# A Macaron layer on one core: the front of the second router pass starts during the first attention, and two groups of instructions are pinned in the order

## The chip, the cores and the metric

The kernel runs on one core of one Trainium2 chip. A core has a matrix engine (TensorE, PE in the profile, with its weight loads listed as PEld), a vector engine (VectorE, DVE), a scalar engine (ScalarE, ACT), a general engine (GpSimd, POOL), and a sync engine (SyncE, SP) that issues DMAs. The metric is the time of one execution on the device in microseconds (us); lower is better. All data are float32.

## The reference

The input x is 2 sequences of 2048 tokens with 256 channels. The layer is a half-weighted feed-forward part, a causal attention, and the same feed-forward part again with the same weights:

```python
x = x + 0.5 * ffn(layernorm(x))
x = x + attn(layernorm(x), Wq, Wk, Wv, Wo)      # causal, d_k = 128
x = x + 0.5 * ffn(layernorm(x))

def ffn(x):
    xln = ln(x, ln1_w, ln1_b)
    state = xln @ Ws
    x = x + sigmoid(xln @ Wr) * (xln @ Wv) @ Wo
    h = ln(x, ln2_w, ln2_b)
    conf = concat(sigmoid(h @ conf_rwkv.T), sigmoid(h @ conf_trans))   # three experts
    bids = conf * capital_shares * sigmoid(h @ w_diff) + h @ W_aff
    winners = argmax(bids)
    scale = conf[winner] / (conf[winner] + 1e-6)
    out_rw[e] = square(relu(h @ K[e])) @ V[e]          # e = 0, 1; hidden size 1024
    out_gt = (h @ W1 * sigmoid(state @ W2)) @ W3       # the third expert
    return x + select(winners, out_rw[0], out_rw[1], out_gt) * scale
```

The reference computes all experts for all tokens and selects. The kernel sends each token to its winner alone.

## The kernel before, in words

**Tiling.** A tile is 128 tokens on the partitions. A group is 512 tokens (4 tiles, `TB`), a sequence is 4 groups (`GB`). The kernel works on *segments*, one for each sequence and feed-forward part: s0 and s1 in the first part, t0 and t1 in the second. An expert block is 256 tokens (`BLK`).

**The front** (`front`, L747, with `Group`, from L374) does everything of a feed-forward part that comes ahead of the experts. For each group: `start` takes the mean and variance of x with bn_stats and bn_aggr on DVE and has POOL raise them to the power -0.5 (L291), a first guess that two DVE steps refine; `norm1` normalizes and copies x into the token's row (a DMA on SP, L404); `columns` transposes on PE (`ps_t`); `r` and `v` multiply by w_r and w_v (L362, result `ps_p`), take the sigmoid on ACT and form `gate_t` on DVE (L432); `mix` multiplies by w_o (L442, result `acc`); `route` forms the router's sums in two parts (`ps_rc`, copied to `by_col` by ACT); `deviation` and `norm2` are the second norm; `logits` and `choose` find the winner (`wins` on DVE, L525); `rank` counts on PE the tokens ahead (`ps_rank`, L536); `slot` makes each token's place; `move` scatters the group's rows to `by_slot` in device memory with four indirect DMAs from POOL (L567). The generator interleaves these steps over neighbouring groups: group n's choice stands beside group n+1's projections and the start of group n+2. After a segment's last group `finish` makes a steering table (`ps_n`, `steer`) that tells the experts where their blocks begin.

A `Group` has two flags. With `by_exp` the sigmoid of the gate is taken as a tanh on ACT with an extra scale and shift on DVE; with `conf_by_exp` the sigmoid of the confidences is an exp on ACT with an add and a reciprocal on DVE. Both let groups that run beside the softmax use the same activation table as its exp. The `by_exp` argument of `front` says up to which group this holds.

**The experts** (`experts`, L829) run over a list of `Block`s: gt blocks (the third expert), rw blocks (the first two) and half blocks. SP reads a block's place out of the steering table and loads its rows (`rows_in`, `load_rows`) and, for rw, its weights (`w_k`, `w_e`). `ready` scales a row on DVE (L975) and normalizes it on ACT; `columns` transposes on PE (`ps_bt`, L846); `first` multiplies by the expert's first matrix (L862) and forms `hid` or `gated` (L994) on DVE; `second` multiplies back (`acc`, L877), and the result rows `res` (L902) are scattered from POOL (L910). The rows of block n+1 are made ready within block n.

**Attention** (`attention`, L1067) takes one sequence. `qkv` transposes and projects; `scores` multiplies queries by keys (`ps_s`, L1125), finds the row maximum on DVE (L1134) and the exp on ACT (`prob`, L1141); `values` transposes the probabilities (`ps_pt`, L1165), copies them to SBUF alternately on ACT (L1170) and DVE (L1172) as `p_tr`, and multiplies by v (`ps_o`, L1178); `sums` copies `ps_o` to `o_t` (L1194), multiplies by Wo (`ps_out`, L1200) and adds into x. Group n of a sequence is final once its `sums` are done; the scores of group n+1 are interleaved with the values of group n.

**What sets the order.** The parts are Python generators. Their interleaving gives the order in which instructions are traced; a scheduler then orders each engine's instructions by priority and readiness as it estimates them, so an instruction can move ahead of others traced before it. Two calls hold one back: `tc.keep_in_program_order(ins)` keeps it behind everything traced before it on its engine, and `tc.issue_after(ins)` keeps it behind a given instruction. Only the first feed-forward part's first front is laid out by hand (`tc.manual_schedule`) on PE, DVE and ACT.

The whole program runs: the front of s0; the front of s1 interleaved with the experts of the first part; x read back from device memory (`x_mid`) with its statistics (`normed`, L1286, through `normalize` and `moments`); a conditional block (L1056) that is normally skipped; the first attention on t0; the second attention on t1 with the front of t0 between its steps; the experts of the second part, with the front of t1 between them. `advance(steps, n)` takes n steps of a generator, `run` takes all, `interleave(main, side, steps, every)` takes `steps` steps of the side for each `every` of the main.

In the kernel before, the lines that place the second front are these (8 front steps for each 9 steps of the second attention, then the rest until t0 is placed, then 10 steps more):

```python
        run(attention(work, t0["x"], [r[:, :, YN : YN + C] for r in t0["rows"]]))
        following = front(front_pool, [t0, t1], by_exp=GB)
        interleave(attention(work, t1["x"]), until_placed(following, t0), 9, 8)
        advance(following, AHEAD)
```

Of the kernel before, what the change touches and what calls it, by code (L numbers as in the profile page):

```python
# [17 lines left out]
C = 256  # L18
# [37 lines left out]
def run(steps):  # L56
    for _ in steps:
        pass
# [20 lines left out]
def kernel(ctx: ExitStack, tc: tile.TileContext, a: dict, out: bass.AP):  # L79
    nc = tc.nc  # L80
    x_in = a["x"].flatten_outer_dims()
    out = out.flatten_outer_dims()
    B, T, _ = a["x"].shape
# [192 lines left out]
    def moments(src, landing=False):  # L276

        stats = small.tile([P, TB, 6], F32, name="stats")
        mv = small.tile([P, TB, 2], F32, name="mv")
        for t in range(TB):  # L280
            ins = nc.vector.bn_stats(stats[:, t, :], src[:, t, :])
            if landing and t == 0:
                tc.keep_in_program_order(ins)
        for t in range(TB):
            nc.vector.bn_aggr(mv[:, t, :], stats[:, t, :])
        return mv
# [81 lines left out]
    groups = []  # L368

# [3 lines left out]
    class Group:  # L373
# [136 lines left out]
        def choose(self):  # L510
# [14 lines left out]
            nc.vector.scalar_tensor_tensor(  # L525
                wins[:, 1, :], wins[:, 0, :], 1.0, wins[:, 2, :], ALU.is_lt, ALU.subtract
            )
# [52 lines left out]
    def segment(b, bufs, prior=None, waited=False):  # L580
# [5 lines left out]
        if prior is None:  # L586
# [4 lines left out]
            "moves": groups[-1], "prior": prior, "waited": waited,  # L591
# [155 lines left out]
    def front(work, segs, by_exp=-1, on_move=lambda: None, fill=()):  # L747
# [3 lines left out]
            Group(work, seg, n, (b * GB + n <= by_exp, b * GB + n < by_exp)) for b, seg in enumerate(segs) for n in range(GB)  # L751
        ]

# [6 lines left out]

        todo[0].start()
        run(todo[0].norm1(TB // 2))
        yield
        todo[1].start()
# [8 lines left out]
        for i, this in enumerate(todo):  # L773
# [19 lines left out]
            if further:  # L793
                further.start()
                yield
# [33 lines left out]
    def experts(work, segs, dest, redo=None):  # L829
# [118 lines left out]
        class Block:  # L948
# [36 lines left out]
            def first(self, following=None):  # L985

                if self.kind == "gt":
# [3 lines left out]
                    if following:  # L991
                        following.ready()
# [22 lines left out]
        def pipelined(todo):  # L1015
# [8 lines left out]
            todo[0].ready()  # L1024
            todo[0].columns()
            yield
            for i, block in enumerate(todo):
# [4 lines left out]
                yield from block.first(todo[i + 1] if i + 1 < len(todo) else None)  # L1032
# [34 lines left out]
    def attention(work, x, normed=()):  # L1067

        stat = work

# [120 lines left out]
        def sums(n, ps_o, probs):  # L1191
# [4 lines left out]
            for t0 in range(0, TB, 2):  # L1196
# [6 lines left out]
                for i in range(2):  # L1203
                    t = t0 + i
                    nc.vector.scalar_tensor_tensor(
                        x[n][:, t, :], ps[:, i, :], probs[t][1], x[n][:, t, :], ALU.mult, ALU.add
                    )
            yield
# [106 lines left out]
    with pool("attention", "right") as work:  # L1315
# [4 lines left out]
        run(attention(work, t0["x"], [r[:, :, YN : YN + C] for r in t0["rows"]]))  # L1320
        following = front(front_pool, [t0, t1], by_exp=GB)
        interleave(attention(work, t1["x"]), until_placed(following, t0), 9, 8)
# [50 lines left out]
```

## Time and profile before

| what | value |
|---|---|
| time, median of 3 runs | 898.68 us (897.06 to 899.32) |
| profiled execution | 900.5 us, of which span 898.5 us |
| mean granted PE clock over the span | 0.988 |
| DVE, ACT, POOL busy | 467.4, 320.1, 184.8 us |
| q1 (hardware DMA queue) / q0 (software queue) | 29.0% / 9.5% of 16 engines |
| HBM read and written | 82.47 and 38.68 MB |

The span is the time from the first to the last instruction that the profiler records; the time of an execution is some 2 us more. Busy time is summed over an engine's instructions; matmuls are pipelined, so their printed durations overlap and the distance between starts tells what one costs. In the listings, L12 is line 12 of the kernel, `out<-in` names the tiles, x4 the number of instructions. In a table of stretches each row is one stretch: its bounds and length, then for PE, PEld, DVE, ACT and POOL the busy us and (in brackets) the instructions, then the granted clock of PE, the DMA share and the mean GB/s. In a list of waits, each line gives the waiting instruction, the instruction that released it, and total us, number and mean of the waits.

By the trace, the first feed-forward part's last expert block ends at 338.7 us, the first attention runs from 342.3 to 466.5 us (its first `ps_out` at 395.9), the second with the front of t0 from 466.5 to 637.6 us, and the first rw block of the second part starts at 702.2 us.

### The profile page before, as it was taken

How to read it: one execution, taken by the hardware profiler on the slowest of the kernel's cores; microseconds unless marked ns; L12 is line 12 of the kernel's file. 1: busy time of each engine (PE TensorE's matmuls, PEld its weight loads, DVE VectorE, ACT ScalarE, POOL GpSimd, SP SyncE). 2: the span in 40 equal slices, each digit the busy share in tenths (PEclk: the TensorE clock that was granted, in tenths of full speed). 3: DMA queues.
4: the chain of work that ended last, by engine and by line, in shares of the span. 5: the costliest groups of instructions: out<-in, count | busy, mean ns of one | idle time of the engine just before them, and what ended most of it. 6: DMA issues, size and time to landing. Idle time of an engine off the chain costs nothing. (4 is left out here: it accounts for less than half of the span.)

```text
span 898.5 us, 12471 instructions
## 1 busy us (share of the span) xinstructions
PE 846.5 (94%) x4136; PEld 616.5 (69%) x4136; DVE 467.4 (52%) x1857; ACT 320.1 (36%) x694; POOL 184.8 (21%) x232
## 2 busy tenths in 40 slices
PE   6999899999999998899899999999899899999996
PEld 4556467788878895545456556556566688888885
DVE  3688757333345445478532687675776532333322
ACT  3332541324344332344533344442352223243221
POOL 3145245111032211000000102022323410122101
PEclk9999999999999999999999999999999999999998
DMA  9425637647188543000000001021375654539642
GB/s 308 150 102 194 224 142 264 216 136 264 49 293 296 171 142 100 0 1 1 0 1 1 1 0 71 24 95 42 127 279 182 242 191 161 177 95 333 199 164 70
DMA packets 66370, 123.71 MB, mean 138 GB/s; under 512 B 4718, under 2 KB 44526, under 8 KB 66288
## 3 DMA queue, kind: packets, MB, share of 16 engines
q1 hardware_dynamic: 55856, 87.46, 29.0%
q0 software_dynamic: 8384, 33.70, 9.5%
q10 hardware_dynamic: 2048, 1.58, 0.6%
q8 instruction: 37, 0.61, 0.3%
q14 instruction: 45, 0.37, 0.1%
HBM read 82.47 MB, written 38.68 MB: 135 GB/s over the span
## 5 line engine op out<-in xcount | busy, mean ns | idle before, releaser
L877 PE MATMUL acc<-w_e,hid 128*128 128x256 f32 x704 | 158.2, 382 | 0.0
L862 PE MATMUL ps_b<-cols,w_k 128*128 128x256 f32 (+1 forms) x768 | 157.3, 363 | 0.0
L862 PEld LDWEIGHTS ps_b<-cols,w_k 128*128 128x128 f32 x768 | 137.4, 191 | 17.1
L877 PEld LDWEIGHTS acc<-w_e,hid 128*128 128x128 f32 x704 | 132.7, 192 | 17.9 <-DVE hid L1004 0.6
L291 POOL TENSOR_TENSOR r<-ve,mhalf 128x4 f32<-128x4 f32 (+1 forms) x40 | 50.9, 1272 | 383.0 <-DVE ve L332 264.4
L1003 ACT ACTIVATE relu<-ps_b 128x512 f32<-128x512 f32 x88 | 52.0, 591 | 179.5 <-PE ps_b L862 155.9
L1004 DVE TENSOR_TENSOR hid<-ps_b,relu 128x512 f32<-128x512 f32 x88 | 60.8, 691 | 84.8 <-ACT relu L1003 79.3
L902 DVE SCALAR_TENSOR_TENSOR res<-acc,rows_in 128x256 f32<-128x256 f32 x68 | 30.0, 478 | 123.9 <-PE acc L877 123.9
L1178 PE MATMUL ps_o<-p_tr,v 128*128 128x512 f32 (+3 forms) x160 | 75.2, 554 | 4.7 <-DVE p_tr L1172 1.9
L567 POOL DMA_INDIRECT by_slot<-rows,slots x64 | 62.5, 977 | 32.0 <-issue 27.0
L1141 ACT ACTIVATE prob<-ps_s,shift 128x512 f32<-128x512 f32 (+2 forms) x80 | 49.0, 621 | 53.8 <-DVE shift L1138 44.5
L1125 PE MATMUL ps_s<-k_t,q_t 128*128 128x512 f32 (+3 forms) x160 | 64.8, 533 | 0.9 <-ACT prob L1141 0.9
L910 POOL DMA_INDIRECT out_dram<-res,where x34 | 33.6, 987 | 155.4 <-DVE res L902 142.3
L362 PE MATMUL ps_p<-y_t,w_r 128*128 128x512 f32 x128 | 63.5, 615 | 0.8 <-ACT y_t L416 0.7
L362 PE MATMUL ps_p<-y_t,w_v 128*128 128x512 f32 x128 | 62.2, 605 | 0.0
L910 POOL DMA_INDIRECT x_mid<-res,where x34 | 33.7, 992 | 133.2 <-DVE res L902 128.0
L442 PE MATMUL acc<-w_o,gate_t 128*128 128x256 f32 x256 | 60.1, 385 | 0.6 <-DVE gate_t L432 0.6
L1165 PEld LDWEIGHTS ps_pt<-ident,prob 128*128 128x128 f32 x272 | 34.1, 143 | 36.9 <-issue 18.8
L1134 DVE TENSOR_REDUCE top<-ps_s 128x1 f32<-128x512 f32 (+2 forms) x80 | 48.4, 607 | 17.2 <-PE ps_s L1125 15.8
L442 PEld LDWEIGHTS acc<-w_o,gate_t 128*128 128x128 f32 x256 | 47.1, 190 | 8.6 <-DVE gate_t L432 1.4
L1125 PEld LDWEIGHTS ps_s<-k_t,q_t 128*128 128x128 f32 x160 | 29.9, 193 | 32.8 <-issue 24.7
L354 ACT ACTIVATE cols<-ps_bt,lnp 128x256 f32<-128x256 f32 (+1 forms) x96 | 47.2, 554 | 13.2 <-PE ps_bt L846 12.9
(219 smaller groups left out, 1128.1 us busy)
## 6 DMA issues: line engine op xcount, KB each, us to landing
w_k<-in_K_rwkv_dram SPq DMA_DIRECT2D x24, 1024.0 KB, 5.3
w_e<-in_V_rwkv_dram SPq DMA_DIRECT2D x24, 1024.0 KB, 5.8
rows_in<-by_slot SPq DMA_DIRECT2D x20, 516.0 KB, 6.6
rows_in<-by_slot SPq DMA_DIRECT2D x12, 772.0 KB, 6.6
rows<-in_x_dram SPq DMA_DIRECT2D x8, 512.0 KB, 5.9
by_slot<-rows_in SPq DMA_DIRECT2D x3, 772.0 KB, 10.5
x_mid<-rows_in SPq DMA_DIRECT2D x1, 2048.0 KB, 15.8
rows<-x_mid SPq DMA_DIRECT2D x4, 512.0 KB, 5.1
```

Of the source, the lines that this page charges most:

```text
L291: guess = nc.gpsimd.tensor_tensor(r0[:, 0:n, :], ve[:, 0:n, :], mhalf[:, 0:n, :], ALU.pow)
L362: nc.tensor.matmul(ps, lhsT=w[:, k, m * P : (m + 1) * P], rhs=src_t[:, k, :], start=k == 0, stop=k == KC - 1)
L442: nc.tensor.matmul(acc[:, i, :], lhsT=self.gate_t[:, k, t * P : (t + 1) * P], rhs=w_o[:, k, :], start=k == 0, stop=k == KC - 1,)
L567: nc.gpsimd.indirect_dma_start(out=by_slot, out_offset=bass.IndirectOffsetOnAxis(ap=self.slots[:, t : t + 1], axis=0), in_=self.rows[:, t, :],
L862: nc.tensor.matmul(ps[:, j, :], lhsT=w[:, k, (m0 + j) * P : (m0 + j + 1) * P], rhs=cols[:, k, :], start=k == 0, stop=k == KC - 1,)
L877: nc.tensor.matmul(acc[:, i, :], lhsT=src[:, j, i * P : (i + 1) * P], rhs=w[:, j, :], start=j == 0, stop=j == n - 1,)
L910: ins = nc.gpsimd.indirect_dma_start(out=dest, out_offset=bass.IndirectOffsetOnAxis(ap=where[:, i : i + 1], axis=0), in_=res[:, i, :], in_ ...
L1003: nc.scalar.activation(relu, ps, AF.Relu)
L1004: self.made = nc.vector.tensor_mul(self.mid[:, j : j + step, :], ps, relu).ins
L1125: nc.tensor.matmul(ps[:, :w], lhsT=seq["q_t"][:, qi * P : (qi + 1) * P], rhs=seq["k_t"][:, c * TG : c * TG + w], start=True, stop=True,)
L1141: nc.scalar.activation(prob[:, c * TG : c * TG + w], ps[:, :w], AF.Exp, bias=shift, scale=ATTN_SCALE, accum_out=sums[:, c : c + 1],)
L1178: nc.tensor.matmul(ps_o[:, i0 * P :], lhsT=seq["v"][:, j, :], rhs=p_tr[:, i0 * P :], start=j == 0, stop=j == blocks - 1,)
```

## The change

In words:

1. In `moments`, all four bn_stats of statistics taken with `landing=True` (those of the x that is read back from `x_mid`) are kept in program order, not the first alone.
2. The front keeps in `lately["chosen"]` the last instruction of the latest `choose`. The first block of the experts, and the block that is made ready within the first block, are made ready behind that instruction on DVE.
3. Each segment has a counter `attended`. It is 4 (all groups) by default; for t0 and t1 it starts at 0 and attention raises it after each group's `sums`. The front starts a group only when the counter is past it, and otherwise yields a step.
4. The front of t0 and t1 is created ahead of the first attention. It advances on every second step of the first attention and on every step of the second, then runs until t0 is placed, and then 10 steps more as before.
5. The groups that use tanh for the gate are now all of t0 and the first three of t1 (before: t0 and the first of t1); those that use exp for the confidences are t0 and the first of t1 (before: t0). The front of the first part uses neither, as before.

```diff
@@ -279,7 +279,7 @@
         mv = small.tile([P, TB, 2], F32, name="mv")
         for t in range(TB):
             ins = nc.vector.bn_stats(stats[:, t, :], src[:, t, :])
-            if landing and t == 0:
+            if landing:
                 tc.keep_in_program_order(ins)
         for t in range(TB):
             nc.vector.bn_aggr(mv[:, t, :], stats[:, t, :])
@@ -366,6 +366,7 @@
 
 
     groups = []
+    lately = {}
 
 
     RW_AT, GT_AT, HALF_AT, MORE_AT, STEER = accumulate(POS, POS, POS, SQ, 1)
@@ -522,9 +523,9 @@
             wins = self.wins = sort_pool.tile([P, E, TB], F32, name="wins")
             nc.vector.tensor_tensor(wins[:, 0, :], bids[:, 0, :], most[:, 1, :], ALU.is_ge)
             nc.vector.tensor_tensor(wins[:, 2, :], bids[:, 2, :], most[:, 0, :], ALU.is_gt)
-            nc.vector.scalar_tensor_tensor(
+            lately["chosen"] = nc.vector.scalar_tensor_tensor(
                 wins[:, 1, :], wins[:, 0, :], 1.0, wins[:, 2, :], ALU.is_lt, ALU.subtract
-            )
+            ).ins
             for t in range(TB):
                 at = self.n * TB + t
                 nc.vector.tensor_add(upto[:, :, at + 1], upto[:, :, at], wins[:, :, t])
@@ -588,7 +589,7 @@
         groups.append(f"moves{b}_{len(groups)}")
         return {
             "b": b, "ids": ids[:, b, :], "bufs": bufs, "rows": [], "in_rows": [], "x": [], "upto": upto, "moved": [],
-            "moves": groups[-1], "prior": prior, "waited": waited,
+            "moves": groups[-1], "prior": prior, "waited": waited, "attended": GB,
         }
 
     def finish(seg):
@@ -744,12 +745,17 @@
         nc.vector.reduce_max(at[:, 5:6], flags, axis=AX.X)
         nc.vector.tensor_copy(steer[:, MORE_AT : MORE_AT + 1], at[:, 5:6])
 
-    def front(work, segs, by_exp=-1, on_move=lambda: None, fill=()):
+    def front(work, segs, by_exp=-2, on_move=lambda: None, fill=()):
+
 
 
         todo = [
-            Group(work, seg, n, (b * GB + n <= by_exp, b * GB + n < by_exp)) for b, seg in enumerate(segs) for n in range(GB)
+            Group(work, seg, n, (b * GB + n < by_exp + 2, b * GB + n < by_exp)) for b, seg in enumerate(segs) for n in range(GB)
         ]
+
+        def attended(group):
+            while group.seg["attended"] <= group.n:
+                yield
 
         def at(i):
             return todo[i] if 0 <= i < len(todo) else None
@@ -758,9 +764,11 @@
             group.move()
             on_move()
 
+        yield from attended(todo[0])
         todo[0].start()
         run(todo[0].norm1(TB // 2))
         yield
+        yield from attended(todo[1])
         todo[1].start()
         todo[0].columns()
         yield
@@ -791,6 +799,7 @@
                 yield
 
             if further:
+                yield from attended(further)
                 further.start()
                 yield
             if late:
@@ -982,14 +991,14 @@
                     self.cols_y = columns(self.rows, YN, 0)
                 self.cols = columns(self.rows, X1, 1)
 
-            def first(self, following=None):
+            def first(self, following=None, early=False):
 
                 if self.kind == "gt":
                     sig = work.tile([P, 2, BLK], F32, name="gt_sig", bufs=1)
                     nc.scalar.activation(sig, several(w_s2, 0, self.cols_y), AF.Sigmoid)
                     yield
                     if following:
-                        following.ready()
+                        following.ready(lately["chosen"] if early else None)
                     self.mid = work.tile([P, KC, BLK], F32, name="gated", bufs=2)
                     self.made = nc.vector.tensor_mul(self.mid, several(later["w_1"], 0, self.cols), sig).ins
                     yield
@@ -1021,7 +1030,8 @@
 
             yield
             yield
-            todo[0].ready()
+
+            todo[0].ready(lately["chosen"])
             todo[0].columns()
             yield
             for i, block in enumerate(todo):
@@ -1029,7 +1039,7 @@
                     todo[i + 1].load_weights()
                 if i + 2 < len(todo):
                     todo[i + 2].load_rows()
-                yield from block.first(todo[i + 1] if i + 1 < len(todo) else None)
+                yield from block.first(todo[i + 1] if i + 1 < len(todo) else None, i == 0)
                 if i + 1 < len(todo):
                     todo[i + 1].columns()
                     yield
@@ -1064,9 +1074,10 @@
                 run(redo())
 
 
-    def attention(work, x, normed=()):
+    def attention(work, seg, normed=()):
 
         stat = work
+        x = seg["x"]
 
         def qkv(made):
             q_t = work.tile([P, T], F32, name="q_t")
@@ -1205,6 +1216,7 @@
                     nc.vector.scalar_tensor_tensor(
                         x[n][:, t, :], ps[:, i, :], probs[t][1], x[n][:, t, :], ALU.mult, ALU.add
                     )
+            seg["attended"] += 1
             yield
 
         seq, probs, left = {}, [], []
@@ -1317,9 +1329,13 @@
             x = front_pool.tile([P, TB, C], F32, name=f"x{n}")
             wait_for(nc.sync.dma_start(x, token_tiles(x_mid, GB + n)).ins, s0["results"] + s1["results"])
             t1["x"].append(x)
-        run(attention(work, t0["x"], [r[:, :, YN : YN + C] for r in t0["rows"]]))
-        following = front(front_pool, [t0, t1], by_exp=GB)
-        interleave(attention(work, t1["x"]), until_placed(following, t0), 9, 8)
+        t0["attended"] = t1["attended"] = 0
+        following = front(front_pool, [t0, t1], by_exp=GB + 1)
+        for n, _ in enumerate(attention(work, t0, [r[:, :, YN : YN + C] for r in t0["rows"]])):
+            advance(following, n % 2)
+        for _ in attention(work, t1):
+            advance(following, 1)
+        run(until_placed(following, t0))
         advance(following, AHEAD)
     expert_pool = ctx.enter_context(pool("experts1", "right"))
     main = experts(expert_pool, [t0, t1], out)
```

## Prediction

> **What bounds the kernel now.** I read the page's first part and its chain first, then a table of stretches around the two attentions, then PE's waits in each stretch, and last how the change reorders each engine's instructions.
>
> ```profile
> PE 846.5 (94%) x4136; PEld 616.5 (69%) x4136; DVE 467.4 (52%) x1857; ACT 320.1 (36%) x694; POOL 184.8 (21%) x232
> ...
> POOL out_dram L910 0%; POOLq L1055 0%
> ```
>
> TensorE (PE) is nearly always occupied and the chain breaks off after one step, so the time has to be read as PE work plus PE standing still. What one matmul really takes is the distance between starts, not its printed duration:
>
> ```profile
> 64.44 1.88 PE L362 MATMUL ps_p<-y_t,w_r 128*128 128x512 f32 x4
> 66.16 1.88 PE L362 MATMUL ps_p<-y_t,w_v 128*128 128x512 f32 x4
> ```
>
> Four records in 1.72 us is 0.43 us for a 512-wide record; by the same reading 0.217 for 256, 0.109 for 128, 0.108 for a transpose, 0.57 for the 16 records of one ps_rc half. The table of stretches (PE, PEld, DVE, ACT and POOL busy us with instruction counts, then the granted PE clock): first attention from its second score group on, second attention with the whole first-segment front beside it, first attention's opening, and the stretch up to the first rw block:
>
> ```profile
> 395.90:466.50 70.60, 65.47 (x257) 37.12 (x255) 43.01 (x144) 31.29 (x82) 4.28 (x3) 1.00 0.00 1
> 466.50:637.60 171.10, 168.02 (x784) 100.33 (x785) 108.40 (x413) 65.61 (x163) 22.37 (x20) 1.00 0.10 38
> 342.30:395.90 53.60, 48.39 (x200) 30.46 (x201) 29.92 (x110) 19.05 (x45) 3.06 (x3) 0.90 0.13 41
> 637.60:702.20 64.60, 60.22 (x362) 40.16 (x362) 46.09 (x250) 25.89 (x52) 25.00 (x24) 1.00 0.58 211
> ```
>
> I counted the records of each stretch by shape and multiplied. First row: 90 records of 512 (38.7), 114 transposes (12.3), 35 of 256 (7.6), 10 of 384 (3.3), 8 of 128 (0.9): 62.7 us of work in 70.6, so 7.9 us of standing still. Second row: 224 of 512 (96.3), 112 of 256 (24.3), 212 transposes (22.9), 80 of 128 (8.7), 16 of 384 (5.2), ps_rc and ps_rank (6.0): 163.4 in 171.1, 7.7 lost although the stretch is more than twice as long. Fourth row, the same way: 57.5 in 64.6, 7.1 lost. The third loses about 13.5, a good part of it through a clock of 0.90. PE's waits in the first row's stretch name what is missing, the softmax chain:
>
> ```profile
> PE ps_pt L1165 <- ACT prob L1141: 1.5, 2, 0.8
> PE ps_o L1178 <- DVE p_tr L1172: 1.4, 2, 0.7
> PE ps_s L1125 <- ACT prob L1141: 0.9, 1, 0.9
> PE ps_out L1200 <- ACT o_t L1194: 0.7, 1, 0.7
> PE ps_o L1178 <- ACT p_tr L1170: 0.6, 2, 0.3
> ```
>
> The reader is to see 5.1 us of named waits with nothing else for PE to do; in the second attention, which has front work between its matmuls, the named waits are 2.5 us in 171.
>
> **The change part by part.**
>
> *The front moves forward.* No matmul is added or removed, so it can pay only by filling PE's gaps. In the new order the first attention holds all of group 0 and group 1 as far as its gates: 16 transposes (1.7), 32 records each of w_r and w_v, 16 instructions in 512 columns (13.7), one w_o set (3.5), two ps_rc halves (1.1), one route transpose (0.1): 20.2 us. It starts after the first ps_out, so the opening (the third row) keeps its 13.5. The work of the first row becomes 62.7 + 20.2 = 82.9. At the second attention's rate, 7.7 lost for 163.4 of work, that loses 3.9 instead of 7.9: **-4.0**. Bounds: its later part alone (531.2 to 637.6 us) loses 1.8 in 106.4, which would give 1.4 lost and -6.5; other side under the first rival.
>
> *What the move drags along.* Norms of group 0 and 1 already stand there before (ACT rows at 407 and 429 us). New on VectorE (DVE): the rest of group 0 and half of group 1, about 12 us, and the statistics of the second sequence, 12 more bn_stats with their bn_aggr, 0.37 and 0.11 us each, with the small steps 6 us: 43.0 becomes 61 in some 87, 70%, against 61% now. ACT gains some 7 us in 31.3. The copies of x into rows (SP, L404) keep their order and SP is otherwise idle here. POOL keeps its scatter order, its power roots only move. The scatters of the second segment's rows stand behind all of the first experts', as before.
>
> *Second attention.* It had 59.0 us of front; group 1's second half, 2, 3, the second segment's group 0 and half its group 1 make some 48.5. With less to cover the query/key/value part, where 6.2 of the 7.7 are lost (466.5 to 531.2), I add **+0.8** (ends: -1 and +3).
>
> *The stretch after it.* 46.6 us of work instead of 57.5; two of its waits, 2.5 us for by_col and 1.5 for gated, belong to two transitions, one of which now lies under attention: **-1.0** (ends -4 and +2; the by_col wait's releaser is not shown, so I take little of it). The steering table is ready some 15 us of PE work before the last ps_out, so the first rows can be issued earlier; SP now reads 12 table entries instead of 10 ahead of them. The ten took 643.4 to 649.8, so +1.3, hidden behind that lead. Without the lead it would be 1.3 late for rows needed some 18 us after.
>
> *Tanh for two more groups.* 4 more tensor_scalar at 0.42 and one exp/add/reciprocal of 0.7: 2.4 us on DVE in stretches where it has over 18 us free; nothing on PE. If DVE were full there, up to 2.4. The activation-table loads stay at four of 1.28.
>
> *First rows keep their place.* Now rows_in is scaled on DVE before the first segment's last choice; it waits for its transfer with the choice behind it:
>
> ```profile
> DVE rows_in L975 <- DMA rows_in<-by_slot: 2.4, 1, 2.4
> ...
> PE ps_rank L536 <- DVE wins L525: 1.1, 1, 1.1
> ...
> PE acc L442 <- DVE gate_t L432: 0.6, 1, 0.6
> ```
>
> With the choice first both PE waits go: **-1.7** (ends 0 and -1.7; the rows are used 8 us later and have landed at 100.0 us).
>
> *Read-back statistics keep their place.* Three of four bn_stats floated ahead and waited for x_mid with a gate product behind them:
>
> ```profile
> DVE stats L281 <- DMA rows<-x_mid: 3.1, 1, 3.1
> ...
> PE acc L877 <- DVE gated L994: 1.6, 1, 1.6
> ```
>
> They now stand some steps later, after the 257 us landing: **-1.6** (ends -2 and +0.5, four statistics in a row being 1.5 us before a hid product whose PE has several tiles in hand).
>
> [...] The rows say POOL's power root makes DVE wait 1.9 us in the first row's stretch and 1.6 in the second, and none of it appears among PE's waits. [...] I follow the rows, since the second attention has this very mixture. What the trace cannot show is the new order's own alignment.
>
> **Sum.** -4.0 + 0.8 - 1.0 - 1.7 - 1.6 = **-7.5 us**. It is made against the profiled execution (span 898.5, 900.5 us with 2.0 outside it), which stands 1.8 us over the median of 898.68; I take the saving from the median: **891.2 us**. About 0.3%, 2.7 us, is what a measurement of this kernel can tell from no change.
>
> **The rivals.**
>
> *Slower: softmax held up, and the clock with it.* Place: DVE's queue in the first attention after 396 us. [...] Between 372 and 392 us PE stood still for some 4.5 us in pieces of 0.4 to 1.8, and the granted clock of the opening stretch is 0.90, so 0.10 x 53.6 = 5.4 us lost; after 396 it is 1.00. [...] It decides from about 4 us of PE waits inside 20 us. Against it: the second attention's 1.00 beside the same front.
>
> *Filled here, given back later.* The second attention and the expert stage lose 4 to 7 us more because 10.9 us less front covers them (the ends above, +3 and +2): 896 to 901.
>
> *Only the two pins pay.* The scheduler's order in the first attention fills nothing: -3.3, 895.4 us.
>
> **How the numbers follow.** Main case 0.56 (885 to 895); only the pins 0.08; given back 0.13, counted as no change; slower 0.23. So faster 0.64, same 0.13, slower 0.23. The unknown ends on the good side, -6.5, -1, -4, -1.7 and -2, together would be 883.5; all of them at once is unlikely, so the range is 884 to 902, which leaves out most of the slow case's upper half.
>
> **What would show it.** Right: PE's named waits after the first ps_out of the first attention fall from 5.1 to about 2 us with the clock at 1.00; the second attention ends some 6 us later than before on the clock of the run (637.6 minus 3.3, minus 4.0, plus 9.7 us of work brought forward, plus 0.8: about 641), yet the first rw block begins near 695 instead of 702; the waits of 2.4 and 3.1 us on DVE are gone. Wrong: a granted clock under 1.00 after 396 us, ps_pt or ps_o waiting for p_tr behind a power root, rows_in waited for by DVE after the second attention, or a stretch before the first rw block that still takes over 60 us.

## The result, and the profile after

The changed kernel is slower: 907.24 us (median of 15 runs) against 899.17 us for the kernel before, measured beside it (15 runs). The ratio is 1.0075, 95% interval 1.0047 to 1.0103. The forecast was 891.2 us with a range of 884 to 902. Its profiled execution took 902.34 us with a span of 900.6 us, at the low end of its runs (900.58 to 915.26 us). The ratio leaves out the three runs above 914 us, which are more than 1.5% over the fastest, and is therefore smaller than that of the two medians; the granted clock of the three (0.973 to 0.975) is that of the slowest runs kept.

The table of stretches of the changed kernel, with the same marks as before: first attention from its second score group on, second attention, first attention's opening, and the stretch up to the first rw block (columns as before: bounds, length, PE, PEld, DVE, ACT, POOL, granted clock, DMA share, GB/s).

```profile
393.10:480.40 87.30, 84.56 (x354) 48.20 (x352) 59.12 (x217) 36.52 (x92) 9.07 (x7) 1.00 0.00 1
480.40:651.60 171.20, 160.28 (x760) 96.96 (x760) 107.69 (x447) 66.36 (x167) 27.26 (x25) 0.99 0.15 56
341.70:393.10 51.40, 46.80 (x201) 30.12 (x202) 22.94 (x71) 17.18 (x41) 0.00 (x0) 0.93 0.13 42
651.60:704.30 52.70, 51.23 (x290) 34.27 (x289) 37.60 (x199) 21.31 (x42) 19.61 (x19) 0.97 0.46 162
```

By the prediction's count, the first row's stretch has 20.2 us more PE work than before; it is 16.7 us longer (87.3 against 70.6): the front does fill it. The last row's stretch has 10.9 us less work and is 11.9 us shorter. The opening, the third row, is 2.2 us shorter (51.4 against 53.6); it has one stretch of half clock fewer, worth 1.7 us. The second row is what the forecast missed: by its own count it has 10.5 us less work, and it takes 171.2 us where it took 171.1. PE's waits there say why. First the waits of the first attention after its first `ps_out`, then those of the second attention's first 65 us (the third figure of a line is the longest single wait, not the mean):

```profile
PE ps_pt L1176 <- ACT prob L1152: 0.9, 1, 0.9
PE ps_o L1189 <- DVE p_tr L1183: 0.7, 1, 0.7
PE ps_s L1136 <- ACT prob L1152: 0.5, 1, 0.5
PE ps_pt L1176 <- ACT by_col L479: 0.4, 1, 0.4
PE ps_t L348 <- DVE p_tr L1183: 0.3, 1, 0.3
```

```profile
PE ps_pt L1176 <- ACT prob L1152: 3.5, 2, 1.8
PE ps_t L348 <- DVE xn L325: 2.0, 1, 2.0
PE ps_t L348 <- ACT x_t L1100: 0.7, 1, 0.7
PE ps_o L1189 <- DVE total L1161: 0.7, 1, 0.7
PE ps_pt L1176 <- ACT p_tr L1181: 0.6, 1, 0.6
PE ps_t L348 <- ACT xn L320: 0.4, 1, 0.4
PE ps_t L348 <- DVE x_t L1099: 0.2, 1, 0.2
```

The first attention's named waits fell from 5.1 to 2.8 us. The second attention's opening, which had 1.3 us of them before (466.5 to 531.2 us), now has 8.1; the rest of it went from 1.2 to 2.7. The waits of the opening are of two kinds. PE waits for `xn`, the normalized x of the second sequence; and it waits twice for 1.8 us between a group's last scores and its first transposes. The timeline of VectorE shows the first kind, first in the kernel before, then in the changed one:

```profile
348.50 1.41 DVE L281 BATCH_NORM_STATS2 stats<-x 128x6 f32<-128x256 f32 x4 [2.57 <-DMA x<-x_mid]
...
355.46 0.73 DVE L325 TENSOR_SCALAR xn<-x,mv,rstd 128x256 f32<-128x256 f32 x2
```

```profile
459.82 0.39 DVE L281 BATCH_NORM_STATS2 stats<-x 128x6 f32<-128x256 f32 x1
...
482.05 0.73 DVE L325 TENSOR_SCALAR xn<-x,mv,rstd 128x256 f32<-128x256 f32 x2
```

Before, the second sequence's first groups were normalized by 357 us, at the start of the first attention. Now their statistics come at its end and `xn` at 482 us, after its last `ps_out`, when PE has nothing else. PE's timeline shows the second kind, before and after, at the start of value group 0 of the second attention, where the values of the first 512 queries begin:

```profile
505.28 1.02 PE L1125 MATMUL ps_s<-k_t,q_t 128*128 128x512 f32 x2
506.24 0.64 PE L468 MATMUL ps_rc<-gate_t,route_g 128*32 128x128 f32 x16
506.81 1.11 PE L348 MATMUL ps_t<-ident,rows 128*128 128x128 f32 x8
508.14 1.70 PE L1165 MATMUL ps_pt<-ident,prob 128*128 128x128 f32 x7 [0.22 <-ACT y_t L416]
```

```profile
520.06 1.02 PE L1136 MATMUL ps_s<-k_t,q_t 128*128 128x512 f32 x2
520.92 0.71 PE L1176 MATMUL ps_pt<-ident,prob 128*128 128x128 f32 x5
523.39 0.44 PE L1176 MATMUL ps_pt<-ident,prob 128*128 128x128 f32 x2 [1.76 <-ACT prob L1152]
524.40 0.44 PE L1176 MATMUL ps_pt<-ident,prob 128*128 128x128 f32 x2 [0.57 <-ACT p_tr L1181]
```

Before, a `ps_rc` half and eight transposes of the front lay between the last score and the transposes that need its exp. Now nothing does: the same front, earlier by one and a half groups, has steps without PE work at this place. The kernel before shows what such a bare start costs, in its first attention, which had no front beside it:

```profile
373.92 0.44 PE L1165 MATMUL ps_pt<-ident,prob 128*128 128x128 f32 x2 [1.76 <-ACT prob L1141]
```

**Two parts of a run's time.** Every run lists its span and its mean granted clock. Span times clock is taken here as the time at full clock, and span times (1 - clock) as the loss to the clock. This is bookkeeping: it charges a stretch at half clock with half its length even where PE had nothing to do, as in the last stretch of every run, which lies behind the last matmul (some 2.4 us in the trace of the kernel before). All means below are of these two parts, with 1.96 standard errors; for six to nine runs a 95% interval is a fifth to a third wider than that. A stretch that a trace shows at half clock, ahead of that last one, is called a dip.

The runs come in five sets, each with its own runs of the kernel before (set 1 is the measurement above, which lists these parts for the changed kernel alone). In sets 2 and 4 the kernel before takes 880 us at full clock, in sets 3 and 5 it takes 886; sets 2 and 3 ran on the same chip, so the chip is not the reason. The traces of the changed kernel differ in how late expert rows land: in set 3's PE waits 3.3 us for `rows_in` around 157 us, in set 4's not at all. Kernels are compared within a set.

| set | kernel | runs | full clock | lost to the clock |
|---|---|---|---|---|
| 1 | changed | 12 | 886.7 ±0.7 | 17.8 ±2.3 |
| 3 | before | 51 | 886.3 ±0.4 | 12.3 ±0.5 |
| 3 | changed | 7 | 887.8 ±1.3 | 19.4 ±2.5 |
| 4 | before | 43 | 879.8 ±0.5 | 11.9 ±0.8 |
| 4 | changed | 14 | 880.3 ±1.0 | 11.1 ±1.2 |
| 5 | before | 23 | 886.7 ±0.7 | 13.2 ±0.8 |
| 5 | changed | 9 | 886.7 ±1.1 | 18.3 ±2.0 |

At full clock the change is worth nothing (0 to +1.5 us) where 7.5 us had been forecast. Of the sets in which both kernels list their parts, it is slower in sets 3 and 5 alone, and there by the clock (+7.1 and +5.1 us; -0.8 in set 4).

### The profile page after: what moved, and what is told of

Its sections match the earlier page's. It is cut to its first block, busy times and chain, and to the rows that moved or that the text cites. A ratio compares the mean times of both kernels' runs of the same rounds, so it can differ in the third digit from the quotient of the medians.

```text
span 900.6 us, 12482 instructions
## 1 busy us (share of the span) xinstructions
PE 847.4 (94%) x4136; PEld 617.8 (69%) x4136; DVE 467.2 (52%) x1863; ACT 319.8 (36%) x694; POOL 185.2 (21%) x232
## 5 line engine op out<-in xcount | busy, mean ns | idle before, releaser
L871 PEld LDWEIGHTS ps_b<-cols,w_k 128*128 128x128 f32 x768 | 136.5, 190 | 16.7
L354 ACT ACTIVATE cols<-ps_bt,lnp 128x256 f32<-128x256 f32 (+1 forms) x96 | 47.0, 552 | 17.8 <-PE ps_bt L855 17.2
L1176 PE MATMUL ps_pt<-ident,prob 128*128 128x128 f32 x272 | 43.4, 277 | 10.0 <-ACT prob L1152 7.7
```

Of the source, the lines that this page charges most:

```text
L871: nc.tensor.matmul(ps[:, j, :], lhsT=w[:, k, (m0 + j) * P : (m0 + j + 1) * P], rhs=cols[:, k, :], start=k == 0, stop=k == KC - 1,)
L1176: nc.tensor.transpose(ps[:, i * P : (i + 1) * P], probs[i][0][:, j * P : (j + 1) * P], ident)
```

## The experiments

**The two pins alone**, on the kernel before (set 2; ratio 0.9977, interval 0.9960 to 0.9994).

```diff
-            if landing and t == 0:
+            if landing:
...
-            nc.vector.scalar_tensor_tensor(
+            lately["chosen"] = nc.vector.scalar_tensor_tensor(
...
-                        following.ready()
+                        following.ready(lately["chosen"] if early else None)
...
-            todo[0].ready()
+            todo[0].ready(lately["chosen"])
```

> The kernel before with the two pins alone (read-back statistics, first rows); the front stays where it was. The prediction had -1.7 for the first rows and -1.6 for the statistics, 3.3 together: a ratio of 0.9963 to before. The trace of the changed kernel speaks for less: the choice no longer waits behind rows_in, but where the statistics' wait of 3.1 us went, PE now waits 1.5 us for rows_in and 0.7 for gated. By that reading the first rows bring -1.7 and the statistics nothing: 0.998. If the loss of the changed kernel comes from the pins after all, this run is at 1.004 or more.

877.9 ±0.5 us at full clock against 880.0 ±0.5, so -2.1; 11.9 us lost, as before. In this set the pins are a small gain. By subtraction, across sets, the moved front alone costs 2 to 4 us at full clock. The run does not say what the pins do to the clock in sets 3 and 5, where the changed kernel loses to it: they were run alone in sets 2 and 4 only.

**The statistics' pin alone**, on the kernel before (set 4; ratio 0.9987, interval 0.9970 to 1.0004).

```diff
-            if landing and t == 0:
+            if landing:
```

> The kernel before with the pin of the read-back statistics alone. The prediction had -1.6 us for it. The traces say that a wait for rows_in (1.5 us) and one for gated (0.7) take the place of the one removed, so 0 at full clock (within 0.5); both pins together gave -2.2 at full clock, and the rest is then the first rows' (-1.7 predicted).

878.5 ±0.6 against 879.8 ±0.5 at full clock: -1.3. The expectation of 0 (within 0.5), read from one pair of traces, was wrong, and the prediction's -1.6 was about right. The first rows' part is what is left of 2.1, some -0.8 across two sets.

**Norms of the second sequence ahead**, on the changed kernel (set 2; ratio 1.0000, interval 0.9985 to 1.0015).

```diff
+            if n == AT_STEP:            # 3
+                for i in range(2):
+                    xn = work.tile([P, TB, C], F32, name="xn", bufs=2)
+                    begun.append((xn, normalize(xn, t1["x"][i], name="_ahead")))
+                    next(begun[i][1])
+            if n == AT_STEP + 24:
+                for _, steps in begun:
+                    run(steps)
...
-        for _ in attention(work, t1):
+        for _ in attention(work, t1, begun=begun):
```

> The changed kernel, with the statistics and the norm of the second sequence's first two groups taken within the first attention (steps 3 and 27), under tile names of their own. Theory 'late norms': in the changed kernel the second attention opens with its x not normalized; PE waits 2.0, 0.7, 0.4 and 0.2 us and a clock dip of 1.7 us follows at 485 us. They go, and the run is 3 to 5 us faster than the changed kernel (ratio to before 1.002 to 1.004). Theory 'thin cover': the loss sits in the softmax of the second attention's start, which has 7.2 us of front beside it instead of 13.2; then this run gains at most the 3.3 us less what the softmax gives back, and stays at 1.006 or more.

The small statistics tiles of these norms have names of their own (`_ahead`), in lines left out above.

**The front held back from step 40 of the first attention**, on the changed kernel (set 2; ratio 0.9994, interval 0.9973 to 1.0015).

```diff
-            advance(following, n % 2)
+            advance(following, n % 2 if n < HOLD else 0)      # HOLD = 40
```

> The changed kernel, with the front stopped at step 40 of the first attention, so that group 1's w_r and w_v (6.9 us of PE) open the second attention instead of filling the end of the first. Theory 'thin cover': the waits of the second attention's first 65 us fall from 10 us to about 6, the first attention's rise by 1 to 2, so 2 to 4 us faster than the changed kernel (ratio to before 1.003 to 1.005). Theory 'late norms': the opening still waits for xn, PE's first 3.3 us and the dip stay, and nothing is won (1.006 to 1.009).

**Both edits together** (set 2; ratio 1.0013, interval 0.9990 to 1.0035; 14 runs).

> Both at once: norms of the second sequence's first two groups ahead, and the front held from step 40 of the first attention. If the two causes are separate, their gains add: 5 to 8 us faster than the changed kernel, ratio to before 0.998 to 1.002. If either is the whole of it, this run is no better than the better of the two. In both theories the mean granted clock over the runs rises from 0.979 to 0.985 or so, since the gaps ahead of the dips are gone; if the clock stays at 0.979, the dips have another cause.

Full clock 879.0 ±0.7, 880.2 ±0.7, 879.9 ±0.9 against 880.0 ±0.5 of before. Set 2 has no run of the changed kernel, so no theory of these three expectations is decided by a ratio; they only say that none beats before, and that the two edits don't add up: the held front opens the second attention with `w_r` and `w_v`, but at value group 0's start there is again nothing between scores and transposes:

```profile
508.77 0.71 PE L1177 MATMUL ps_pt<-ident,prob 128*128 128x128 f32 x5
511.24 0.44 PE L1177 MATMUL ps_pt<-ident,prob 128*128 128x128 f32 x2 [1.76 <-ACT prob L1153]
```

The wait in the held kernel's timeline is the 1.76 us of the changed one. This points to where the front lies rather than how much of it there is.

**The changed kernel again** (set 3; ratio 1.0089, interval 1.0056 to 1.0121).

> The changed kernel again, beside the kernel before on one chip, so that the span and the mean granted clock of every run of both can be set against each other. Theory 'clock': span times clock (the time at full clock) is the same as before's within 1 us, and all the extra time is in span times (1 - clock): about 17 us against 12. Theory 'late work': span times clock is 5 us or more above before's, the clock like before's. First measurement 1.0075; expected 1.004 to 1.009.

+1.5 us at full clock and +7.1 us of clock: the first theory, nearly (it had 1 and 5).

**Front steps shifted onto the two starts**, on the changed kernel (set 3; ratio 1.0020, interval 0.9998 to 1.0041).

```diff
+ALIGN = {5: 0, 6: 0, 7: 4, 9: 0, 10: 0, 11: 4, 12: 0}
...
-        for _ in attention(work, t1):
-            advance(following, 1)
+        for n, _ in enumerate(attention(work, t1)):
+            advance(following, ALIGN.get(n, 1))
```

> The changed kernel with the same number of front steps in the second attention, but shifted by up to three steps, so that w_r of group 2 lies between the last scores and the first transposes of value group 0, and w_v, w_r, w_v between those of value group 1. Theory 'alignment': the two waits of 1.76 us and their followers (0.6 and 0.7) go, 3.5 to 4.8 us at full clock, and the dips with them, 2.5 us: 5 to 7 us faster than the changed kernel. Theory 'thin cover' (too little front for the whole opening): the waits appear a few us later instead; gain at most 2.5.

882.8 ±0.8 against 887.8 ±1.3 at full clock: -5.0, and -1.4 of clock (18.0 ±1.6 against 19.4 ±2.5). In PE's timeline of this kernel the same place now reads:

```profile
519.57 1.02 PE L1137 MATMUL ps_s<-k_t,q_t 128*128 128x512 f32 x2
520.43 1.88 PE L363 MATMUL ps_p<-y_t,w_r 128*128 128x512 f32 x4
522.15 1.19 PE L1177 MATMUL ps_pt<-ident,prob 128*128 128x128 f32 x7
```

The reader is to see four records of `w_r` where PE stood for 1.76 us. At value group 1's start the wait of 1.76 us is gone too; the waits for `xn` are still there.

**Both repairs, shifted steps and norms ahead: the two diffs together** (set 3; ratio 0.9968, interval 0.9949 to 0.9987).

> The shifted steps together with the norms of the second sequence's first two groups taken within the first attention. If late norms and alignment are the two halves of what went wrong, all of PE's named waits in the second attention's first 65 us but 2 us go: 9 to 12 us faster than the changed kernel, a ratio to before of 0.994 to 0.997. If the norms, moved ahead, only push the first attention's softmax back (the run with norms ahead alone had a dip at 410 us that the changed kernel has not), the gain over the shifted steps alone is under 2 us.

880.1 ±0.8 at full clock: another -2.7, and -2.1 of clock. Of what PE waits for in the second attention's opening, this is left:

```profile
PE ps_route L498 <- ACT p_tr L1183: 0.6, 1, 0.6
PE ps_o L1191 <- DVE p_tr L1185: 0.6, 1, 0.6
PE ps_t L350 <- DVE rows L1218: 0.2, 1, 0.2
```

The two repairs together take 11.2 us off the changed kernel (7.7 at full clock, 3.5 of clock). The clock still takes 15.9 ±1.1 us against 12.3 ±0.5 of before.

**The norms at step 42 instead of 27** (set 4, 6 runs: ratio 0.9873, interval 0.9844 to 0.9903; set 5, 12 runs: ratio 0.9964, interval 0.9944 to 0.9984).

```diff
-            if n == AT_STEP + 24:
+            if n == 42:
```

> The shifted steps and the norms ahead, with the norms at step 42 of the first attention instead of 27. At step 27 they stood on VectorE beside the row maxima of value group 1's start, and PE waited 1.7 us for prob at 409 us, with a dip at 410 us; at step 42 both go: 1 us at full clock and 0.7 x 1.71 = 1.2 us of clock, so 2 us less than with step 27 and a ratio to before of about 0.994. If VectorE is as full at step 42, the wait moves there and the ratio stays at 0.997.

> The version with shifted steps and norms at step 42 again, since the last set gave only 6 runs of it (ratio 0.987, 7.6 us lost to the clock against 11.9 of before). With its gaps closed it has three dips left in the trace; expected ratio 0.986 to 0.994, and a narrow spread of its runs in either kind of set. If its loss to the clock is above before's in a set where the changed kernel loses 19 us, the gain of the last set was luck of position.

This version beats both kernels in both sets: 873.4 ±0.7 against 879.8 at full clock in set 4, 881.4 ±0.9 against 886.7 in set 5, so -6.4 and -5.3. The clock gives 4.3 us more in set 4 (7.6 against 11.9) and takes 2.3 more in set 5 (15.5 against 13.2). So the gain at full clock holds. By the second expectation's own measure the clock's part of set 4's gain was luck of position; the ratio of set 5 is above the expected 0.986 to 0.994, and its runs lose 10.7 to 19.7 us to the clock, which is no narrow spread.

**Useless matmuls in the two gaps**, on the changed kernel, in the second attention alone, result unread (set 3; ratio 1.0087, interval 1.0061 to 1.0113).

```diff
         for n in range(GB):
+            if warm and n < 2:
+                ps = p_mm.tile([P, TG], F32, name="ps_w", tag="mm")
+                for _ in range(2):
+                    nc.tensor.matmul(ps, lhsT=seq["q_t"][:, (n * TB + 3) * P : (n * TB + 4) * P],
+                                     rhs=seq["k_t"][:, n * TG : (n + 1) * TG], start=True, stop=True)
...
-        for _ in attention(work, t1):
+        for _ in attention(work, t1, warm=True):
```

> The changed kernel with useless matmuls (the last score block twice again, 4 records of 0.43 us, result unread) just ahead of the first transposes of the second attention's first two value groups, where PE otherwise waits 1.76 us for prob at 522 and 535 us. They fill PE's time and bring nothing forward. Theory 'clock': each of these gaps, laid over windows of 3.41 us, leaves PE busy under half of a window at 0.7 to 0.8 of all phases, and the window after it runs at half clock (1.71 us lost); filling them saves 1.45 x 1.71 = 2.5 us and the clock rises by 0.003, though nothing else is faster. Theory 'waits only': useless work saves nothing (0), or costs up to 1 us.

887.8 and 19.1 ±1.9 against 887.8 and 19.4 ±2.5. The expected 2.5 us is not seen, and with these intervals it can't be excluded either. In its trace both waits are filled.

**Useless matmuls in three gaps**, the kernel just shown with one more place, behind the first attention's last sums (set 4; ratio 1.0003, interval 0.9980 to 1.0025), beside the changed kernel once more (ratio 0.9992, interval 0.9969 to 1.0014).

```diff
+            if last and n == GB - 1:
+                ps = p_mm.tile([P, TG], F32, name="ps_w", tag="mm")
+                for t in range(4):
+                    nc.tensor.matmul(ps[:, 0:C], lhsT=o_t[:, t * P : (t + 1) * P], rhs=later["wa_o"], start=True, stop=True)
```

> The changed kernel once more, as the yardstick of this chip for the three runs beside it. Span times clock within 2 us of before's, and 7 us more lost to the clock, as in the last measurement; ratio 1.005 to 1.010.

> The changed kernel with useless matmuls in three gaps: the two before value groups 0 and 1 of the second attention, and four instructions of 256 columns (1.7 us) after the first attention's last ps_out, in the 2.0 us that PE waits for xn. Theory 'clock': the third gap has a dip behind it in every profile of the changed kernel (485 to 488 us), the other two by their length at 0.7 of all phases; filled, 2.4 dips of 1.71 us go, 4.1 us, all of it in span times (1 - clock), while span times clock stays as it is. Theory 'waits only': both parts stay within 1 us. With two gaps filled the loss to the clock was 19.1 us against 19.5, which spoke for the second.

Neither expectation was met. The changed kernel was to lose 7 us more to the clock than before and lost 0.8 less; the fills were to save 4.1 us: 880.9 and 11.2 ±1.3 against 880.3 and 11.1 ±1.2, no gain. In this set 9 of the changed kernel's 14 runs lost 10.7 us, so there was little to save at the two starts. In the trace of the filled kernel the third gap's wait for `xn` is down from 2.0 to 0.3 us, but a dip at 484 us stays: the waits of 0.4, 0.7 and 0.4 us that follow it among the first transposes leave PE busy for 1.9 us of the step ahead of it. The fill closed the longest of these gaps and not the ones that the dip stands behind.

**The grid.** Laid over each other, the dips of the traces show a grid. In the kernel before, they start at 149.5, 344.1, 374.8, 388.4 and 712.7 us: 57, 9, 4 and 95 steps of 3.413 us apart. In each of the 18 profiled executions all of them lie on one such grid, and each lasts for one or two whole steps. One example, two neighbouring steps of the changed kernel with the shift described below (columns as above; PE's busy time comes first, the clock third from the end; the rows begin 0.1 us ahead of the grid, hence 0.51):

```profile
530.84:534.25 3.41, 1.20 (x6) 0.72 (x7) 2.00 (x7) 1.26 (x3) 0.00 (x0) 1.00 0.00 0
534.25:537.66 3.41, 3.41 (x8) 1.57 (x6) 0.96 (x3) 0.00 (x0) 0.00 (x0) 0.51 0.00 0
```

PE was busy for 1.20 us of the first row (1.30 on the grid itself), and the next step ran at half clock. Counted over all 18 executions from 24 to 870 us, where the earlier step was at full clock:

| PE busy in a step of 3.41 us | steps | next step at half clock |
|---|---|---|
| under 1.3 us | 44 | 44 |
| 1.3 to 1.6 | 22 | 20 |
| 1.6 to 1.9 | 47 | 23 |
| 1.9 to 2.3 | 89 | 20 |
| 2.3 and more | 4125 | 0 |

So in these traces about half a step of idling cost up to half of the next step, 1.71 us, and whether a gap of 2 us did so depended on where it lay on the grid: behind the wait of 1.76 us that ends at 532.5 us in the shifted kernel stands the half-clock step shown here, and behind the same wait of the unshifted kernel (until 523.4 us in set 1's trace) none. Sliding the grid over the changed kernel's trace and taking the shares of the table, the two starts (13.6 us apart, just 4 steps) would dip at 0.7 of all positions, as an estimate. In the four traces of the changed kernel neither does.

**The gaps moved by half a step, and moved and filled**, on the changed kernel, in the second attention's projections, result unread (set 5; shift: ratio 1.0113, interval 1.0086 to 1.0141, 6 runs; shift and fill: 1.0079, interval 1.0055 to 1.0104, 9 runs; changed kernel beside them: 1.0051, interval 1.0027 to 1.0075, 9 runs).

```diff
+                if late and n == 1:
+                    ps = p_mm.tile([P, TG], F32, name="ps_w", tag="mm")
+                    for _ in range(2):
+                        nc.tensor.matmul(ps, lhsT=later["wa_q"][:, 0, :], rhs=x_t[:, 0, :], start=True, stop=True)
```

> The changed kernel as the yardstick of this set. Both theories: ratio to before between 0.999 and 1.009, as in the sets before. In the last set it lost 11 us to the clock, most of its runs exactly 10.7 us (4 or 5 dips and the end), in two others 19 us. If most runs agree with each other again, the loss is low; if they spread, it is high.

> The changed kernel with two useless 512-column matmuls (4 records, 1.72 us, half a window of 3.41 us) in the second attention's projections, which move all later gaps by half a window. Theory 'grid': a gap costs half a clock window only where it lies well in a fixed grid of windows; in the last set's trace the windows began 0.5 us ahead of the span of starts that would have dipped (514.4 to 516.6, and the same 13.6 us later), so both gaps were just missed. Moved by 1.72 us they are hit: where the changed kernel's runs agree at 10.7 us lost, this one loses 14 us; where they spread, the mean stays as it is. Span times clock rises by 1.7 us. Theory 'waits only': the loss to the clock stays the same in either case.

> The same shift, and the two gaps ahead of value groups 0 and 1 filled with useless matmuls. Theory 'grid': with the gaps filled there is nothing to hit, and the loss is 3.4 us below that of the shift alone where that one's gaps are hit. Theory 'waits only': as the shift alone, within 1 us.

The loss to the clock was 18.3 ±2.0 (changed), 20.9 ±2.8 (shifted) and 17.0 ±1.9 (shifted and filled); at full clock 886.7, 889.7 and 889.8, so the useless work cost 3.0 us, not 1.7. The 2.6 us between changed and shifted are not clear of the intervals. Filling takes 3.9 us off the shifted kernel's loss, near the grid's 3.4, but the intervals overlap, and in the shifted kernel's trace only one of its dips stands behind a gap that was filled. That one stands behind the very gap that was to be hit (534.3 us, shown above); in no trace of the unshifted changed kernel is there one at this place.

## Why the prediction was wrong, point by point

- **The front fills the first attention (-4.0): right.** 82.9 us of work in 87.3 is 4.4 lost, against 7.9: -3.5. (Its "32 records each of w_r and w_v" are 16 and 16; the 13.7 us stand for the 32 together.)
- **POOL's roots in DVE's queue: rightly left out of the sum.** The slow case, with its chance of 0.23 and its place in the range, counted 6.0 us of them as reaching PE; that was the author's estimate, and no run shows the term. In the first attention DVE waits 3.9 us in all for three roots, and little of it reaches PE. Behind the first (1.0 us, until 400.5 us) DVE runs without a pause to the row maximum whose exp PE then waits for (0.5 us, until 404.5); behind the third (1.1 us, until 452.3) stands a softmax copy for which PE waits 0.3 us; behind the second (1.8 us) PE waits for nothing. That is 0.8 us at most, and PE's waits as a whole fell.
- **Second attention, +0.8 (ends -1 and +3): the step that failed.** By the prediction's own count it lost 7.7 us for 163.4 of work before; now 18.3 for 152.9, so +10.6. The named waits give 8.3 of it (6.8 in its opening, 1.5 after) and a dip 1.7. The term was taken from how much front is left there. What counted was which steps of it fall at the two starts (repaired: -5.0 us at full clock) and that the second sequence's norms, done by 357 us before, had slid to 482 us (repaired: -2.7, and some 2 us more of clock; a dip stands behind these waits in all four traces of the changed kernel, and in none of the five with the norms ahead). The prediction had seen the statistics move and had entered them as DVE's load, "12 more bn_stats"; it did not ask who waits for them. It had also seen the price of a bare start, PE's 4.5 us of standing still between 372 and 392 us, but charged it to softmax copies held up in the first attention.
- **The stretch after it (-1.0): right**, 6.1 us lost (a dip among them) against 7.1.
- **The pins (-1.7 and -1.6): half right.** Together -2.1 at full clock; the statistics -1.3, the first rows less than said. In the single profile the time up to the first attention is only 0.6 us shorter.
- **Sums that do not come out.** The prediction puts 20.2 us of front into the first attention and takes 10.5 and 10.9, together 21.4, out of the other two stretches. Its split of the second attention's 7.7 us into 6.2 and 1.8 gives 8.0; the records give 4.3 up to 531.2 us and 3.4 after it, and 11.7 rather than 13.5 lost in the opening. Counted record by record at its spacings, the four stretches lose 9.1 (opening), 5.0, 17.8 and 5.1 us now, where they lost 11.7, 8.1, 7.7 and 6.8. With the 0.6 us ahead of them this is the 2.1 us between the two spans. Only the first of these slips enters the sum, with 1.2 us at most.
- **The sum.** At full clock the failed step takes all of the -7.5: 0 to +1.5 was measured. With its two causes repaired and the norms placed well, -5.3 to -6.4 comes back, most of what had been forecast.
- **The rivals.** "Given back later" named the right stage and put +3 on it, a third of what it was. The slower rival had the right second half, the clock, at the wrong place: it looked for it behind DVE's roots after 396 us, where one of the four traces of the changed kernel has a dip (410.9 us, set 5), behind PE waits of 0.9 and 0.7 us with no root in DVE's queue just ahead of them. Its measure, 4 us of waits inside 20, is not what decides: one step with less than 1.3 us of PE work was enough, in 44 of 44 cases. The forecast itself had no term for the clock, though the trace of before showed each of its dips behind a gap of PE (0.83 to 1.91 us of PE work in the step of 3.41 us ahead of each). That is the larger part of the loss against before in the sets where it can be told: +7.1 us in set 3 and +5.1 in set 5.
- **What stays open.** In set 4 the changed kernel lost no more to the clock than before, in sets 3 and 5 much more; why is not shown. The two starts are not seen to be the reason: no trace of the changed kernel has a dip there, and the stretch in which PE waits for the norms has one in set 4's trace as in the others. Of the fills, that of set 5 speaks for the starts and those of sets 3 and 4 do not. The one trace of the kernel before has 5 half-clock steps; those of the changed kernel have 6 (set 1), 8 (set 3), 5 (set 4) and 10 (set 5). Among those that sets 3 and 5 have more are one or two behind the wait for the norms, one after 700 us, and one or two in the first feed-forward part (158 and 265 us), which the moved front does not touch and the pins do. No run has the pins alone in a set like these, and there is no trace of before in them, so the pins' part in the clock's loss is untested. What held the second sequence's norms back, the order of priorities or the four shared buffers of the small statistics tiles, was not separated: the repair gave them names of their own and an earlier place at once.

## What to carry to other kernels

Filler work that is moved to one stage leaves another: ask at which waits it stood there, not only how much of it is left, and look for what the scheduler had floated into the gap that is now filled. When an instruction moves late, follow its result to the one who reads it before counting it as load. And read span and granted clock apart: a kernel can be the same at full clock and still slower, because the clock can charge a gap a second time (here one of 1.76 us, with a step of 3.41 us at 0.51 behind it).

## What was not expected of the hardware

In each of the 18 traces the dips lie on one grid of 3.413 us from the first of them to the last (149.5 to 712.7 us in the kernel before), and one step with little PE work was enough for one: 44 of 44 steps with under 1.3 us of it were followed by a half-clock step, and none of 4125 with 2.3 us or more. And one kernel's time at full clock differed by 6 to 7 us between sets (880 and 886 us for the kernel before), on one chip too (sets 2 and 3). That is more than most of the changes tried here, so only runs of the same set can be compared.
